# Gathers released in three batches a step instead of at eleven instructions, and a new order for the last steps of a graph attention kernel

## The chip, the cores and the metric

The kernel runs on one core of a Trainium2 chip. A core has five engines, each with an instruction queue of its own: TensorE (PE) for matrix products, VectorE (DVE) and ScalarE (ACT) for elementwise work, GpSimd (POOL), here used almost only to issue gathers, and SyncE (SP), which issues plain DMAs. They run side by side and meet at semaphores. The metric is device microseconds of one execution; lower is better.

## The reference

A graph attention layer over 3125 nodes of 128 features and 100000 edges sorted by destination; each edge has one of 5 relations, each relation its own weights for 8 heads of 16.

```python
for r in range(R):
    mask = edge_types == r
    q = jnp.einsum('eh,khd->ekd', x_dst, W_Q[r])
    k = jnp.einsum('eh,khd->ekd', x_src, W_K[r])
    v = jnp.einsum('eh,khd->ekd', x_src, W_V[r])
    logits = (q * k).sum(-1) / scale + attn_bias[r][None, :]
    ...
    exp_l = jnp.where(mask[:, None], jnp.exp(masked_logits - max_v[dst]), 0.0)
    sum_exp = jax.ops.segment_sum(exp_l, dst, num_segments=n)
    attn = exp_l / (sum_exp[dst] + 1e-12)
    out = out + jax.ops.segment_sum(attn[:, :, None] * v, dst, num_segments=n)
out = out.reshape(n, HIDDEN) @ out_proj_w.T + out_proj_b
h = out + node_embeddings
```

`h` is normalised over its features (with gamma and beta), the input is added, and the sum is normalised again.

## The kernel before

**Tiling.** Edges are cut into 782 tiles of 128 (`NTILE`), four tiles to a group, three groups to a step. There are 66 steps (`NST`); the first and the last have two groups. Before the loop, keys and values of all nodes and relations are computed and written to a table in HBM (`kv_d`). In the loop each tile needs the 128 rows of its edges' sources: one indirect DMA on the POOL queue, "a gather" (L836), which reads them into a ring of four steps (`kv_early` for three of them, `kv_late` for one). One tile in most steps needs no gather, since its rows are computed on PE (`early_*`, L1041 to L1067), so a step has 11 gathers; in all there are 719 at L836. Another 63 (L371) come before them.

**A step k of the loop** (L1375 on): `products` (L933) and `logits` (L991) on DVE use the gathered keys; `turn_logits` turns the scores on PE (L1023); `norm` (L1169 to L1173) and `relations` (L1209) finish step k-2; `spread_q` (L911) brings the queries of step k+1 to their edges; `weigh` (L1118) multiplies the gathered values of step k-1 with their weights; two scans (L1073, L1077) and `less_max` (L1087) take the maximum over each destination; `exps` (L1095) follows on ACT, `turn_exps` (L1102) on PE, and `weights` (L1112) on ACT ends the step. Between these stand three `places` on ACT (L1131, L1135: one-hot matrices of destinations) and three `sums` on PE (L1147, L1152: the sums over destinations of step k-1, one group each), taken by `place_next` and `sum_next`.

**The leaves.** The order of each engine's instructions is the order of the program, and a step writes it out by hand. POOL would run ahead as far as the ring lets it; what holds it is a leave. `gather(leave, n)` (L832) issues the next n gathers, and each of them waits for the instruction `leave`. `point(k, j, leave)` (L846) is called eleven times a step, j from 0 to 10, each time with an instruction that has just been written: j = 6 the products, 7 the copy `weights` of the step before (L1112), 8 the logits, 9 and 10 the first and last of `norm`, 0 the product of `weigh`, 1 the last matmul of `spread_q`, 2 and 3 the scans, 4 the DVE comparison of `spot`, 5 the last `places`. How many gathers are due is a formula:

```python
at = k + (j + 1) / POINTS
at += KV_LEAD - (KV_LEAD - KV_LOW) * min(max(at / (NST - 3), 0.0), 1.0)
```

All gathers of the steps up to `at` are issued, so the lead over the step that runs is 3 steps at the start and falls evenly to 2 at the end. (k, 6) to (k, 10) are called in the loop's iteration k+1, (k, 0) to (k, 5) in iteration k. In the text (k, j) is that point, and its gathers are its batch.

**The end.** After the loop the last step (`k = 65`, L1473 on) is written out: its products in two pieces (`piece`), `turn_logits`, `weigh` and `norm` of the steps before, the sums of steps 64 and 65 (`ahead_g`, `g`), and then the last three blocks of nodes (`rest`, 22 to 24): `project` (L1239), `residual` (L1266), `roots` (L1273, on ACT), `norms` (L1290 to L1318) and `store_z`.

Of the kernel before, what the change touches and what calls it, by code (L numbers as in the profile page):

```python
# [19 lines left out]
P = 128  # L20
# [126 lines left out]
def windowed_path(  # L147
# [177 lines left out]
    rsum = keep("rsum", [P, WN])  # L325
    lo = load.tile([1, NGR], F32, name="lo")
# [473 lines left out]
    qe = ps.tile([P, T * G3, H], F32, name="qe")  # L800
    fin = ps.tile([P, 4 * P], F32, name="fin")
# [30 lines left out]
    def gather(leave=None, n=1):  # L832
        for q in sum(tiles, [])[len(issued) :][: max(n, 0)]:
            ((kv, at, _),) = runs(q, q + 1)
            behind(
                nc.gpsimd.indirect_dma_start(  # L836
                    out=kv[:, at, :], out_offset=None, in_=kv_d[:, :],
                    in_offset=bass.IndirectOffsetOnAxis(
                        ap=idx[:, q % T, q // T : q // T + 1], axis=0
                    ),  # L840
                ),
                leave,
            )
            issued.append(q)

    def point(k, j, leave):  # L846
        at = k + (j + 1) / POINTS
        at += KV_LEAD - (KV_LEAD - KV_LOW) * min(max(at / (NST - 3), 0.0), 1.0)
        whole = min(int(at), NST)
        n = sum(len(t) for t in tiles[:whole])  # L850
        if whole < NST:
            n += int((at - whole) * len(tiles[whole]) + 1e-6)
        gather(leave, n - len(issued))
# [373 lines left out]
    def lifted(b):  # L1227
        n = min(P, N - b * P)
        nc.vector.tensor_tensor(
# [22 lines left out]
    def shifted(b):  # L1252
        n = min(P, N - b * P)
        if ("mv", b) not in live:
            live["mv", b] = pair()
            nc.vector.memset(live["mv", b], 0.0)
        xb = xn[:, b, :]
        nc.vector.tensor_tensor(xb[:n], xb[:n], beta_t[:n], op=ALU.add)

    def residual(b):  # L1260
# [4 lines left out]
        h = flow.tile([P, H], F32, name="h", bufs=1)  # L1265
# [4 lines left out]
    def roots(b, c0=0, c1=2, last=False):  # L1270
        sd = flow.tile([P, 2], F32, name="sd")
# [12 lines left out]
    def norms(b):  # L1284
# [30 lines left out]
        if b and c1 == 2:  # L1315
            n = min(P, N - (b - 1) * P)
            z = flow.tile([P, H], F32, name="z")
# [57 lines left out]
    for k in range(NST - 1):  # L1375
# [83 lines left out]
        sum_next()  # L1459
# [21 lines left out]
    live["lt", k] = lt = ps.tile([P, T * GE // 2], F32, name="lt")  # L1481
    for i in range(LASTG):
# [21 lines left out]
    weights(k)  # L1504
    sums(ahead_g[2])
    places(g[1])
    room = qe.rearrange("p n h -> p (n h)")
# [17 lines left out]
    f = starts(first, G0[k], G0[k + 1], ACTE)  # L1525
# [5 lines left out]
    sums(g[1])  # L1531
    last_norm(lt[:, None, :PW], lt[:WR, None, PW : PW + HEADS], n)
    project(rest[1])
# [521 lines left out]
```

## Time and profile before

| | us |
| --- | --- |
| median of 3 runs | 1020.38 |
| lowest and highest of them | 1020.12, 1023.06 |
| profiled execution, its own time | 1029.88 |
| span of the profiled execution | 1028.1 |

Times in the profile are counted from the first instruction of the profiled execution. PE is busy 92% of the span, DVE 87%, POOL 73%, ACT 69%. A row of the timeline gives start, duration, engine, line, operation, out<-in with shapes, how many instructions were merged (x), and in brackets the idle time of the engine before it and what ended that. "issue" means that nothing shown was waited for. In the groups of instructions the last columns are busy time, mean duration in ns, and idle time before with what ended most of it.

### The profile page before, as it was taken

The numbers are of one execution on the slowest core, as the hardware profiler recorded it, in microseconds if no ns is written. First come the engines' busy times: TensorE is split into PE (matmuls) and PEld (weight loads), VectorE is DVE, ScalarE is ACT, GpSimd is POOL, SyncE is SP. The second block draws the span as 40 slices with busy tenths as digits, with TensorE's granted clock in tenths as the row PEclk, the third lists the DMA queues.
The fourth block names the chain that finished last, engine by engine and source line by source line (L and its number), as shares of the span: only waits on it lengthen the run. The fifth ranks groups of instructions, "written<-read, shape, count | busy, mean of one in ns | idle before, by whom it ended". The sixth has DMA issues, their size and how long they took to land.

```text
span 1028.1 us, 21159 instructions
## 1 busy us (share of the span) xinstructions
PE 943.1 (92%) x6981; PEld 730.2 (71%) x6981; DVE 899.3 (87%) x1520; ACT 713.6 (69%) x1947; POOL 748.4 (73%) x793
## 2 busy tenths in 40 slices
PE   7995699999999999999999999999999999999896
PEld 3553578787777777777777777777777777777675
DVE  3665699899989998999999998999898999999895
ACT  2443368687777777777777777878777677877672
POOL 7777777777777777777777777777777777777730
PEclk9997599999999999999999999999999999999985
DMA  8997666666656666665666665666666566676620
GB/s 196 357 348 253 174 173 189 173 187 185 176 167 193 193 181 184 183 181 160 194 191 185 182 190 156 188 186 192 171 193 192 155 190 184 171 194 173 162 60 11
DMA packets 99077, 189.48 MB, mean 184 GB/s; under 512 B 19117, under 2 KB 59521, under 8 KB 98842
## 3 DMA queue, kind: packets, MB, share of 16 engines
q0 software_dynamic: 36528, 98.42, 37.8%
q1 hardware_dynamic: 61240, 88.74, 26.0%
q10 hardware_dynamic: 1194, 0.92, 0.4%
q8 instruction: 56, 0.92, 0.4%
q14 instruction: 59, 0.48, 0.2%
HBM read 157.61 MB, written 30.40 MB: 183 GB/s over the span
## 4 chain that ended last, share of the span: by engine, by line
DVE 35%; PE 26%; DMA 21%; issue 9%; ACT 4%; POOL 3%; DVEq 0%; ACTq 0%; SPq 0%; POOLq 0%
DMA kv_early<-kv_d,idx 14%; DVE qe L991 7%; PE both L1152 5%; DVE kv_early L933 5%; DMA kv_late<-kv_d,idx 5%; PE qe L911 4%; DVE wv L1118 4%; PE pr L508 3%; PE mid L1060 3%; POOL kv_early L836 3%; DVE run L1073 3%; DVE run L1077 3%; PE fin L1209 2%; DVE lx L966 2%; PE lt L1050 2%
## 5 line engine op out<-in xcount | busy, mean ns | idle before, releaser
L836 POOL DMA_INDIRECT kv_early<-kv_d,idx x543 | 515.9, 950 | 168.5 <-issue 85.9
L1152 PE MATMUL both<-wv,at 128*125 128x136 f32 x1552 | 269.4, 299 | 1.4 <-ACT at L1135 1.4
L1152 PEld LDWEIGHTS both<-wv,at 128*125 128x125 f32 x1552 | 207.9, 190 | 52.9 <-issue 46.0
L1131 ACT ACTIVATE at<-wide_at,nkey 128x125 f32<-128x125 f32 x776 | 245.0, 388 | 0.0
L836 POOL DMA_INDIRECT kv_late<-kv_d,idx x176 | 167.3, 950 | 53.6 <-issue 28.6
L1060 PE MATMUL mid<-wkv,xr 128*128 128x256 f32 x630 | 148.7, 383 | 1.6 <-ACT xr L1054 1.6
L911 PE MATMUL qe<-qw,hot 128*128 128x128 bf16 x2349 | 149.6, 225 | 0.0
L911 PEld LDWEIGHTS <-hot 128*128 128x128 bf16 x2352 | 145.4, 103 | 0.5 <-DVE vio L641 0.4
L1060 PEld LDWEIGHTS mid<-wkv,xr 128*128 128x128 f32 x630 | 116.4, 192 | 15.6 <-ACT xr L1054 2.0
L1135 ACT ACTIVATE at<-at 128x500 f32<-128x500 f32 x194 | 120.3, 620 | 6.1
L933 DVE TENSOR_TENSOR kv_early<-kv_early,qe 128x1536 f32<-128x1536 f32 (+3 forms) x70 | 89.2, 1275 | 25.9 <-DMA kv_early<-kv_d,idx 15.0
L1213 ACT COPY oT<-fin 128x25 f32 x194 | 35.1, 181 | 92.3 <-PE fin L1209 87.4
L1073 DVE TENSOR_TENSOR_SCAN run<-mk,lt 120x640 f32<-120x640 bf16 (+1 forms) x66 | 97.6, 1478 | 1.5 <-PE lt L1023 1.5
L1118 DVE TENSOR_TENSOR wv<-kv_early,mid 128x1536 f32<-128x1536 f32 (+2 forms) x51 | 86.2, 1692 | 12.4 <-PE mid L1060 9.3
L1077 DVE TENSOR_TENSOR_SCAN run<-lt,run 120x576 f32<-120x576 bf16 (+1 forms) x65 | 88.2, 1357 | 2.2
L991 DVE TENSOR_REDUCE qe<-kv_early 128x96 f32<-128x1536 f32 (+2 forms) x65 | 86.7, 1334 | 2.2
L1050 PE MATMUL lt<-diag,xg 128*128 128x512 f32 x252 | 84.1, 457 | 0.0
L1023 PE MATMUL lt<-ident,lx 128*120 128x128 f32 (+2 forms) x396 | 55.2, 277 | 26.8 <-DVE lx L966 10.7
L1023 PEld LDWEIGHTS lt<-ident,lx 128*120 128x120 f32 (+2 forms) x396 | 38.9, 137 | 55.7 <-ACT diag L1044 21.6
L1147 PE MATMUL both<-wv,over 128*5 128x136 f32 x386 | 77.3, 282 | 0.0
L1102 PEld LDWEIGHTS mid<-gather_heads,ls 120*128 120x128 f32 (+1 forms) x528 | 65.1, 194 | 15.0 <-ACT xTq L862 12.6
L1102 PE MATMUL mid<-gather_heads,ls 120*128 120x24 f32 (+1 forms) x528 | 67.4, 265 | 8.9 <-ACT xTq L862 7.5
(210 smaller groups left out, 1337.2 us busy)
## 6 DMA issues: line engine op xcount, KB each, us to landing
kt<-key_d SPq DMA_DIRECT2D x64, 384.0 KB
qw<-q_d SPq DMA_DIRECT2D x196, 96.0 KB
kv_d<-kvs SPq DMA_DIRECT2D x24, 640.0 KB
q_d<-q SPq DMA_DIRECT2D x25, 480.0 KB
mk<-msk_d SPq DMA_DIRECT2D x64, 150.5 KB
kv_early<-kv_d,idx POOLq DMA_INDIRECT x543
kv_late<-kv_d,idx POOLq DMA_INDIRECT x176
out<-z SPq DMA_DIRECT2D x24, 64.0 KB
```

Source lines behind the costliest of these rows:

```text
L836: nc.gpsimd.indirect_dma_start(out=kv[:, at, :], out_offset=None, in_=kv_d[:, :], in_offset=bass.IndirectOffsetOnAxis(ap=idx[:, q % T, q / ...
L911: spread = nc.tensor.matmul(dest[j], hot[:, j * P : (j + 1) * P], qw[:, c, :], start=(c == 0), stop=(c == 2),)
L933: made = nc.vector.tensor_tensor(kv[:, c0:c1, :H], kv[:, c0:c1, :H], qe[:, n:m], op=ALU.mult)
L991: made = nc.vector.tensor_reduce(lg[:, n : n + c1 - c0], heads(kv[:, c0:c1, :H]), AX.X, ALU.add)
L1060: nc.tensor.matmul(rows, xr[:, r * P : (r + 1) * P], wkv[:, r].rearrange("h s c -> h (s c)"), start=(r == 0), stop=(r == R - 1),)
L1073: there = nc.vector.tensor_tensor_scan(run[:n], mk[:n, 1 : WIDE + 1], lt, -BIG, op0=ALU.add, op1=ALU.max)
L1077: back = nc.vector.tensor_tensor_scan(run[:n, SEG:][:, ::-1], masks[:, SEG:][:, ::-1], run[:n, SEG:][:, ::-1], -BIG, op0=ALU.add, op1=ALU.max,
L1102: nc.tensor.matmul(ex.rearrange("p (i t) k -> p t i k", t=T)[:, t], ls[: n * LANES, t * P : (t + 1) * P], gather_heads[: n * LANES, :n], s ...
L1118: return nc.vector.tensor_tensor(heads(wv[:, a:b, :H]), heads(kv[:, at + a : at + b, H:]), ex[:, a:b, :, None].to_broadcast([P, b - a, HEA ...
L1131: nc.scalar.activation(at[:, t, :], row_at[:, :WR], AF.Abs, bias=nkey[:, t, g : g + 1], scale=1.0)
L1135: return nc.scalar.activation(at[:, :n], at[:, :n], AF.Relu, bias=1.0, scale=-1.0)
L1152: nc.tensor.matmul(pp[:WR], at[:, t, :], wv[:, T * i + t, :], start=(t == 0), stop=(t == end))
```

## The change

1. `point` returns at once unless j is 9, 1 or 7, and in `gather` only the first gather of a call gets the leave; the others follow it on POOL's queue. The formula for the number of gathers is as before.
2. In the last iteration of the loop (step 64) the third `sum_next` is left out, and two matmuls on a tile of zeros (`stir`) stand in its place. That group of sums comes after the loop, behind `turn_logits` and `weigh`.
3. After the loop the order is new: `norm`, `relations` and `by_node` of step 63 move behind the scans, the sums of step 64 come later, `places(g[1])` comes ahead of `weights`, `roots(begun)` behind the weighing.
4. The additions of `lifted`, and of `shifted` for the last three blocks, move from DVE to POOL and ahead of the pieces.
5. In the last blocks the second normalisation's roots are taken apart from the first's (`roots(b, 1, 2)` and `roots(b, 0, 1)`), both `residual`s come ahead of the `norms`, and some tiles get more buffers (`h` 2, `sd` 4, `z` 3).

```diff
+    still = keep("still", [P, 2 * P], BF16)
+    nc.vector.memset(still, 0.0)
...
                 leave,
             )
+            leave = None
             issued.append(q)
 
     def point(k, j, leave):
+        if j not in (9,1,7,):
+            return
...
+    def stir(n):
+        for _ in range(n):
+            nc.tensor.matmul(mid[:, P : 3 * P], still[:, :P], still, start=True, stop=True)
...
     def lifted(b):
         n = min(P, N - b * P)
-        nc.vector.tensor_tensor(
+        nc.gpsimd.tensor_tensor(
             ends[b - NT + len(ends)][:n], xn[:n, b, :], lift_t[:n], op=ALU.add
         )
...
     def shifted(b):
         n = min(P, N - b * P)
+        engine = nc.gpsimd if b >= begun else nc.vector
         if ("mv", b) not in live:
             live["mv", b] = pair()
-            nc.vector.memset(live["mv", b], 0.0)
+            engine.memset(live["mv", b], 0.0)
         xb = xn[:, b, :]
-        nc.vector.tensor_tensor(xb[:n], xb[:n], beta_t[:n], op=ALU.add)
+        engine.tensor_tensor(xb[:n], xb[:n], beta_t[:n], op=ALU.add)
...
         turn_exps(k)
         if soon:
             early_turn(k + 2, lt)
-        sum_next()
+        if k < NST - 2:
+            sum_next()
+        else:
+            stir(2)
...
+    shifted(begun)
+    for b in rest[1:]:
+        lifted(b)
+        shifted(b)
     for i in range(LASTG):
         piece(k, i)
     turn_logits(k)
     weigh(k - 1)
-    norm(k - 2)
-    relations(k - 2, fin[:, 3 * P :])
-    sums(ahead_g[0])
+    sum_next()
     places(ahead_g[1])
     places(ahead_g[2])
     places(g[0])
-    sums(ahead_g[1])
-    by_node(k - 2)
+    sums(ahead_g[0])
     scans(k)
     less_max(k)
+    sums(ahead_g[1])
     exps(k)
-    shifted(begun)
+    norm(k - 2)
     residual(begun)
-    for b in rest[1:]:
-        lifted(b)
-        shifted(b)
-    roots(begun, last=True)
     turn_exps(k)
+    relations(k - 2, fin[:, 3 * P :])
+    places(g[1])
     weights(k)
-    sums(ahead_g[2])
-    places(g[1])
...
     for i in range(LASTG):
         weigh(k, i, i + 1)
-    sums(g[0])
+    roots(begun, last=True)
+    by_node(k - 2)
+    sums(ahead_g[2])
     norm(k - 1)
-    relations(k - 1, fin[:, 3 * P :])
-    by_node(k - 1)
     norms(begun)
     store_z(begun - 1)
+    sums(g[0])
+    relations(k - 1, fin[:, 3 * P :])
+    f = starts(first, G0[k], G0[k + 1], ACTE)
+    by_node(k - 1)
+    roots(rest[1], 1, 2, last=True)
...
     sums(g[1])
+    project(rest[1])
     last_norm(lt[:, None, :PW], lt[:WR, None, PW : PW + HEADS], n)
-    project(rest[1])
+    norms(rest[1])
+    store_z(begun)
     last_nodes(mid[:, P:], 0, f[:n])
     last_nodes(lt[:, GE:], n, f[n:])
     residual(rest[1])
-    roots(rest[1], last=True)
+    roots(rest[1], 0, 1, last=True)
     project(rest[2])
+    residual(rest[2])
+    roots(rest[2], 0, 1, last=True)
     norms(rest[1])
-    store_z(begun)
-    residual(rest[2])
-    roots(rest[2], last=True)
+    norms(rest[2])
+    roots(rest[2], 1, 2, last=True)
+    roots(NT, 1, 2, last=True)
     norms(rest[2])
     store_z(rest[1])
-    roots(NT, 1, 2, last=True)
     norms(NT)
     store_z(rest[2])
```

More of the change, by code (lines that the diff above doesn't have):

```diff
@@ L800, in windowed_path @@
     qe = ps.tile([P, T * G3, H], F32, name="qe")
+    room = qe.rearrange("p n h -> p (n h)")
     fin = ps.tile([P, 4 * P], F32, name="fin")
@@ L1264, in residual @@
             xb = ends[b - NT + len(ends)]
-        h = flow.tile([P, H], F32, name="h", bufs=1)
+        h = flow.tile([P, H], F32, name="h")
         nc.vector.tensor_tensor(h[:n], live.pop(("pj", b))[:n], xb[:n], op=ALU.add)
@@ L1270, in roots @@
     def roots(b, c0=0, c1=2, last=False):
-        sd = flow.tile([P, 2], F32, name="sd")
+        sd = flow.tile([P, 2], F32, name="sd", bufs=4)
         if last:
@@ L1316, in norms @@
             n = min(P, N - (b - 1) * P)
-            z = flow.tile([P, H], F32, name="z")
+            z = flow.tile([P, H], F32, name="z", bufs=3)
             nc.vector.tensor_scalar(
@@ L1481, in windowed_path @@
     live["lt", k] = lt = ps.tile([P, T * GE // 2], F32, name="lt")
+    bank = 2 * P * T
+    live["both", k - 1] = room[:, bank : bank + G3 * (PW + HEADS)]
+    shifted(begun)
+    for b in rest[1:]:
+        lifted(b)
+        shifted(b)
     for i in range(LASTG):
@@ L1491, in windowed_path @@
     places(g[0])
-    sums(ahead_g[1])
-    by_node(k - 2)
+    sums(ahead_g[0])
     scans(k)
     less_max(k)
+    sums(ahead_g[1])
     exps(k)
-    shifted(begun)
+    norm(k - 2)
     residual(begun)
-    for b in rest[1:]:
-        lifted(b)
-        shifted(b)
-    roots(begun, last=True)
     turn_exps(k)
+    relations(k - 2, fin[:, 3 * P :])
+    places(g[1])
     weights(k)
-    sums(ahead_g[2])
-    places(g[1])
-    room = qe.rearrange("p n h -> p (n h)")
     live["both", k] = room[:, : G3 * (PW + HEADS + WN)]
@@ L1524, in windowed_path @@
     )
-    f = starts(first, G0[k], G0[k + 1], ACTE)
     n = LASTG - 1
```

## The prediction

> **What bounds the kernel now.** I read the page first: busy shares, slices, the two gather groups.
>
> ```profile
> span 1028.1 us, 21159 instructions
> PE 943.1 (92%) x6981; PEld 730.2 (71%) x6981; DVE 899.3 (87%) x1520; ACT 713.6 (69%) x1947; POOL 748.4 (73%) x793
> ...
> POOL 7777777777777777777777777777777777777730
> ...
> L836 POOL DMA_INDIRECT kv_early<-kv_d,idx x543 | 515.9, 950 | 168.5 <-issue 85.9
> ...
> L836 POOL DMA_INDIRECT kv_late<-kv_d,idx x176 | 167.3, 950 | 53.6 <-issue 28.6
> ```
>
> POOL looks 73% busy and free to spare. It is not: the share is the same in every slice, and the groups hold 719 gathers of 0.95 us with 222.1 us of idle time, 0.31 each. The question is whether that idle time is waiting. The timeline of POOL at the start, where the gathers of L371 have no leave at all, answers:
>
> ```profile
> 9.96 0.95 POOL L371 DMA_INDIRECT xg<-in_x,xi  x1 [0.30 <-issue]
> ```
>
> The same 0.30 us stands before a gather that waits for nothing. So 1.25 us is the pace of a gather, 11 gathers take 13.75 us, and POOL runs at that pace from 86 us (first L836) to 983 us, where the first longer gap comes. A step has 11 gathers; 719 of them at this pace are 899 us, the time from 86 to 985. **POOL is the bound; DVE waits for it in some of the steps**. In this one the last gather of the step starts at 953.28 and its products can start at 957.54, 4.3 us later:
>
> ```profile
> 953.28 0.95 POOL L836 DMA_INDIRECT kv_early<-kv_d,idx  x1 [0.30 <-DVE run L1077]
> ...
> 957.54 1.62 DVE L933 TENSOR_TENSOR kv_early<-kv_early,qe 128x1408 f32<-128x1408 f32 x1 [1.51 <-DMA kv_early<-kv_d,idx]
> ```
>
> A microsecond in which POOL stands still late in the loop is therefore a microsecond at the end.
>
> **The leaves.** What is removed costs nothing: the gap of 0.30 is there with and without a leave. What matters is whether the three leaves that stay come later than POOL does. By the formula of `point` the batch of j = 7 (about 6 gathers) now waits for the ACT copy L1112 that ends step k; its gathers had earlier leaves at points 2 to 7. The batch of j = 9 (2 gathers) waits for the first instruction of `norm`, that of j = 1 (3 gathers) for the last matmul of `spread_q`. I counted the gathers to find each batch's first one and compared its start with the end of its new leave. At the start, batch (1, 7) is the 45th gather (lines view up to it: 33 + 11):
>
> ```profile
> L836 POOL DMA_INDIRECT kv_early<-kv_d,idx x33 | 31.9, 968 | 10.1 <-issue 6.1 <-DMA kv_early<-kv_d,idx 1.2 <-DVE shut L589 0.6
> L836 POOL DMA_INDIRECT kv_late<-kv_d,idx x11 | 10.4, 947 | 3.4 <-issue 2.4 <-DVE wv L1118 0.3 <-DVE run L1073 0.3
> ...
> 134.55 0.24 ACT L1112 COPY wv<-mid 128x96 f32<-128x96 f32 x1 [1.16 <-PE mid L1102]
> ...
> 141.77 0.95 POOL L836 DMA_INDIRECT kv_early<-kv_d,idx  x1 [0.30 <-issue]
> ```
>
> The leave ends at 134.79, POOL arrives at 141.77: 7.0 us to spare, and the wait is free. But the lead falls from 3 steps to 2 over the loop, so the spare time shrinks. The same count at batch (50, 7), gather 576, and (62, 7), gather 706:
>
> ```profile
> L836 POOL DMA_INDIRECT kv_early<-kv_d,idx x432 | 410.7, 951 | 131.7 <-issue 65.8 <-DMA kv_early<-kv_d,idx 14.3 <-DVE both L1169 4.0
> L836 POOL DMA_INDIRECT kv_late<-kv_d,idx x143 | 136.0, 951 | 43.6 <-issue 21.3 <-DMA kv_late<-kv_d,idx 3.4 <-DVE qe L991 1.8
> ...
> 807.98 0.94 POOL L836 DMA_INDIRECT kv_early<-kv_d,idx  x1 [0.30 <-issue]
> 808.83 0.22 ACT L1112 COPY wv<-mid 128x96 f32<-128x96 f32 x1
> ...
> 915.66 0.95 POOL L836 DMA_INDIRECT kv_early<-kv_d,idx  x1 [0.30 <-issue]
> ...
> 918.18 0.24 ACT L1112 COPY wv<-mid 128x96 f32<-128x96 f32 x1 [0.90 <-PE mid L1102]
> ...
> 970.68 0.22 ACT L1112 COPY wv<-mid 128x96 f32<-128x96 f32 x1
> 970.79 0.94 POOL L836 DMA_INDIRECT kv_early<-kv_d,idx  x1 [0.30 <-DVE stats L1249]
> ```
>
> (50, 7): 809.05 against 807.98, POOL would be 1.1 us early. (62, 7): 0.1 early. Of these 13 batches 11 come out early, from 0.1 to 1.5 us, and (58, 7), the rows of 915.66 and 918.18, by 2.8. Behind a waiting gather stand all later ones, and DVE waits for those.
>
> **Sum of the loop.** If the leaves stayed where they are, POOL would be pushed back once, by the largest, 2.8 us. They don't stay: a pushed gather delays the products that wait for it, these delay the next ACT copy, and the next batch waits anew. I carried this through steps 50 to 63 with the trace's own times: a gather starts at the later of its predecessor plus 1.25 and its leave plus 0.15; products start at the later of the former step's DVE work and the landing of their last gather. Stalls of 1.2 (50), 0.3, 0.5, 0.1, 0.9 (55), 1.8 and 1.1 (58), 0.6 (59), 0.3 (61) add up to 6.7 us. Two of the late leaves, in 50 and 58, follow a stretch at half TensorE clock (windows view; columns: length, then busy PE, PEld, DVE, ACT, POOL, then granted clock, DMA share, GB/s):
>
> ```profile
> 800.20:803.60 3.40, 3.40 (x32) 3.40 (x30) 3.33 (x4) 2.38 (x8) 2.53 (x3) 0.50 0.47 100
> 909.40:912.80 3.40, 3.40 (x31) 3.40 (x31) 3.37 (x3) 2.38 (x9) 2.78 (x3) 0.50 0.69 218
> ```
>
> These need not recur; with the distance that other steps have from their products to L1112, the chain gives 4.4 to 5.6, by whether 0 or 0.3 us lie between a leave and its gather. Ends: 0, if later work takes up every stall, and 6.7. I take **+5.0**, since no POOL gap before 983 us is there to take up anything.
>
> The last gathers: before, the last ones are held back at no cost, since DVE is late.
>
> ```profile
> 987.56 0.95 POOL L836 DMA_INDIRECT kv_early<-kv_d,idx  x1 [3.01 <-DVE kv_early L933]
> ...
> 990.06 0.95 POOL L836 DMA_INDIRECT kv_early<-kv_d,idx  x1 [0.30 <-issue]
> 990.15 1.33 PE L911 MATMUL qe<-qw,hot 128*128 128x128 bf16 x21
> ...
> 996.24 0.54 DVE L933 TENSOR_TENSOR kv_early<-kv_early,qe 128x384 f32<-128x384 f32 x1
> ...
> 997.64 0.09 DVE L954 MEMSET lx<- 64x40 f32 x1
> ```
>
> The last one now waits for the matmuls that end at 991.48, starts near 991.6, and with the 4.3 us of the 953.28 row can be used at 995.9, before its use at 996.24: 0, at most 0.5.
>
> **The tail.** These rows carry it (timeline):
>
> ```profile
> 997.16 0.96 PE L1152 MATMUL both<-wv,at 128*125 128x136 f32 x6 [0.74 <-ACT at L1135]
> 999.17 1.32 PE L1023 MATMUL lt<-ident,lx 128*80 128x128 f32 x6
> 999.41 0.19 DVE L1169 TENSOR_SCALAR both<-both 125x24 f32<-125x24 f32 x1
> 1000.56 1.48 DVE L1073 TENSOR_TENSOR_SCAN run<-mk,lt 80x640 f32<-80x640 bf16 x1
> 1000.59 1.47 PE L1209 MATMUL fin<-rsum,o 125*128 125x25 f32 x6
> 1004.07 2.18 PE L1152 MATMUL both<-wv,at 128*125 128x136 f32 x8
> 1007.34 1.72 PE L1102 MATMUL mid<-gather_heads,ls 80*128 80x16 f32 x8
> 1009.34 1.28 DVE L1118 TENSOR_TENSOR wv<-kv_early,mid 128x512 f32<-128x512 f32 x2 [3.05 <-ACT wv L1112]
> 1017.36 0.63 PE L1239 MATMUL fin<-out_wT,oT 128*128 128x128 f32 x2
> ```
>
> PE works nearly without a pause from 997.16 to the projections at 1017.36; the exps turned at L1102 wait in its queue, not for DVE. The change takes a group of sums (997.16 to 999.0) out of the way of the scores and puts it behind them; the scores can start at 997.75 (end of L954) instead of 999.17, and with `norm` moved, the scans start up to 1.15 us earlier (999.41). But the exps still stand behind three groups of sums where two and L1209 stood: two of them took from 1002.06 to 1007.34, 2.65 us each, so 997.75 + 1.3 + 3 x 2.65 give 1007.0, about as before. L1209 (1.5 us) then comes behind them, ahead of the projections. At half clock that is about +1.4, and the new order of the last norms neither gains nor loses more than 0.3. At full clock PE has slack, the earlier scans count, and it is about -0.7. The additions moved to POOL ease a DVE that waits 3.05 us there: 0; POOL has been free since its last gather, 13 us earlier. The two matmuls of `stir` fill the pause of 0.74 ahead of the group that leaves: 0. The zero tile and the extra buffers cost at most a few tenths at the start. Tail: +1.4 to -0.7, I take **0**.
>
> Profiled execution: 1029.88 (span 1028.1 and 1.8 around it) + 5.0 + 0 = 1034.9. The median, 1020.38, is 9.5 lower; the same difference gives **1025.4 us**.
>
> **Rivals.** *The clock returns in the tail (the faster side).* The windows view:
>
> ```profile
> 977.70:981.10 3.40, 3.40 (x31) 3.40 (x31) 3.37 (x3) 2.25 (x9) 2.48 (x4) 0.50 0.32 98
> ...
> 994.70:998.10 3.40, 2.65 (x19) 2.06 (x18) 3.26 (x8) 3.37 (x11) 0.00 (x0) 1.00 0.00 0
> ...
> 1001.50:1005.00 3.50, 3.50 (x15) 2.79 (x16) 3.36 (x6) 2.43 (x8) 0.00 (x0) 0.50 0.03 7
> ```
>
> After a half-filled stretch the clock is 0.50 from 998.1 to the end, though PE is full; after the dense stretch at 977.7 it came back. Sums now run some 8 us on end instead of 5.5. If that lifts the clock near 1004, the PE work left up to 1018.0, 14 us, shrinks by 41% (0.27 us a pass in the 1004.07 row, 0.16 in the 997.16 row), 5.7, less some new waits: -5 against this profile. With +5 that is 1020.4; it decides for faster only if the loop loses under 2 us: 1015 to 1017. The Trainium skill, TensorE: Matmul & The Clock Gate, Part 1, says that the gate judges free-running windows of 3.4 us and opens after a busy one; by that, 8 us always hold a whole window, 5.5 us only by luck. The trace agrees with the length (the half-clock stretches above last 3.4) but shows that a full PE alone isn't enough. For it: the median is 9.5 below this profile, so other executions may already have the clock; then it isn't a gain.
>
> *The leaves don't bind* (the change does nothing in the loop): only the tail, 1019.7 to 1021.8. For: POOL is late up to step 49. Against: 11 of 13 batches after it.
>
> *The stalls grow:* every step from 50 pays 0.7 us or more and the last batch is late: +9, 1029.5.
>
> **Chances.** Forecast 0.57 (own range 1022.5 to 1028), clock 0.20, no binding 0.14, growth 0.09. About 0.3% (3.1 us) is what a measurement can tell from no change: slower needs over 1023.4, nearly all of forecast and growth: 0.62; faster, below 1017.3, is half of the clock case: 0.10; the same 0.28. Range: 1017.5 to 1029.5, with 0.05 left out below and 0.1 above.
>
> **What would show it.** In the changed profile POOL's gaps before L836 stay at 0.30 up to about 800 us and then show some nine of 0.5 to 2 us, released by ACT L1112 and PE L911, in sum 5 (without the last five gathers); the scans of the last step start about 1.1 us earlier after its products; L1102 doesn't, unless the clock is 1.0 there. Wrong it is if POOL never waits, or waits and DVE's gaps before L933 swallow it.

## The result and the profile after

| | before | after |
| --- | --- | --- |
| time, median of 5 runs (us) | 1020.74 (1020.12 to 1023.96) | 1033.68 (1028.04 to 1034.55) |
| ratio, 95% interval | | 1.0104 [1.0081, 1.0128] |
| profiled execution (us) | 1029.88 | 1028.04 |

The change costs 13 us by the medians, where 5 were forecast. The profiled execution of after is the shortest of its five; the other four took 1032.93 to 1034.55 at mean granted clocks of 0.964 to 0.960, the profiled one had 0.969. The profiled execution of before is none of its five, and 9.1 us longer than their median. So the two profiles differ by -1.8 us and the medians by +12.9, and both have to be explained. The chips of all runs behind this section take about 1300 us for the kernel before, not 1020, so what they show is compared only within them.

**The loop after.** The timeline of GpSimd, the rows on which the forecast rests (start, duration, and in brackets the idle time before it and what ended it):

```profile
725.36 0.94 POOL L839 DMA_INDIRECT kv_early<-kv_d,idx  x1 [0.83 <-ACT wv L1118]
...
807.36 0.95 POOL L839 DMA_INDIRECT kv_early<-kv_d,idx  x1 [0.30 <-issue]
...
912.96 0.94 POOL L839 DMA_INDIRECT kv_late<-kv_d,idx  x1 [0.78 <-PE qe L917]
...
917.93 0.94 POOL L839 DMA_INDIRECT kv_early<-kv_d,idx  x1 [1.53 <-ACT wv L1118]
...
942.51 0.94 POOL L839 DMA_INDIRECT kv_early<-kv_d,idx  x1 [1.16 <-PE qe L917]
...
974.08 0.95 POOL L839 DMA_INDIRECT kv_early<-kv_d,idx  x1 [0.30 <-issue]
```

GpSimd now waits for the copy (L1112 before, L1118 now) and for the last matmul of `spread_q` (L911, now L917). Gather 576 starts at 807.36 (807.98 before), gather 706 at 974.08 (970.79 before): 0.6 us ahead has become 3.3 us behind. Counted over the whole loop, without the last five gathers, nine gaps are longer than 0.45 us, from 0.48 to 1.53, and they hold 5.1 us beyond the usual 0.30. The first of them stands before gather 511. Up to there the changed execution had been ahead, as one product and gather 510 show (before, then after; the product at 960.29 is the one that stands at 957.54 in the profile of before):

```profile
682.72 1.62 DVE L933 TENSOR_TENSOR kv_early<-kv_early,qe 128x1408 f32<-128x1408 f32 x1 [0.36 <-DMA kv_late<-kv_d,idx]
...
725.32 0.95 POOL L836 DMA_INDIRECT kv_early<-kv_d,idx  x1 [0.30 <-issue]
```

```profile
680.83 1.62 DVE L939 TENSOR_TENSOR kv_early<-kv_early,qe 128x1408 f32<-128x1408 f32 x1
...
723.59 0.95 POOL L839 DMA_INDIRECT kv_early<-kv_d,idx  x1 [0.30 <-issue]
...
960.29 1.62 DVE L939 TENSOR_TENSOR kv_early<-kv_early,qe 128x1408 f32<-128x1408 f32 x1 [1.52 <-DMA kv_early<-kv_d,idx]
```

GpSimd goes from 1.7 us ahead at gather 510 to 3.3 behind at gather 706: 5.0 us, the sum of the gaps. The eight large products from 627 to 723 us start 0.7 to 2.2 us earlier than before, all of those from 943 us on start 2.5 to 2.8 us later.

**The tail after.** The timeline again, then two stretches of it (length, busy time of PE, PEld, DVE, ACT, POOL, granted clock, DMA share, GB/s):

```profile
998.82 0.54 DVE L939 TENSOR_TENSOR kv_early<-kv_early,qe 128x384 f32<-128x384 f32 x1
...
1001.87 1.47 DVE L1079 TENSOR_TENSOR_SCAN run<-mk,lt 80x640 f32<-80x640 bf16 x1
...
1006.89 1.04 PE L1108 MATMUL mid<-gather_heads,ls 80*128 80x16 f32 x8 [1.31 <-ACT kv_early L1137]
...
1015.52 0.63 PE L1249 MATMUL fin<-out_wT,oT 128*128 128x128 f32 x2
```

```profile
993.00:996.40 3.40, 3.40 (x27) 3.15 (x24) 3.37 (x3) 2.41 (x9) 1.18 (x2) 0.50 0.13 39
...
1000.00:1003.40 3.40, 3.06 (x22) 2.31 (x23) 3.37 (x5) 3.34 (x10) 0.00 (x0) 1.00 0.00 0
```

The last products end 2.6 us later than before (999.36 against 996.78). Since DVE too had been ahead, by 1.6 us in the mean of those eight products, some 4.2 of the 5.1 us lost on GpSimd reached it, and 2.6 are left against before. Why this execution was ahead until then is not shown; 0.3 us of it stand already at the first gather of the loop (85.68 against 86.00). From there to the end it is 26.9 us instead of 31.3. The scans follow the products' start by 3.05 us instead of 4.32, and the clock is 1.0 from 996.4 to 1013.5, where the profile of before has 0.5 from 998.1 to the end. It came back at 996.4, before the last products had ended and so before TensorE came to any of the new order (`stir`, at 999.26). Both executions have full clock for 17.1 us ahead of the last drop (981.1 to 998.1 before); in after this stretch lies later. How much of the 4.4 us is the new order's own is not shown. 2.6 - 4.4 = -1.8: that is the difference of the two profiles.

### The profile page after: what moved, and what is told of

Its sections match the earlier page's. It is cut to its first block, busy times and chain, and to the rows that moved or that the text cites. A ratio compares the mean times of both kernels' runs of the same rounds, so it can differ in the third digit from the quotient of the medians.

```text
span 1026.3 us, 20719 instructions
## 1 busy us (share of the span) xinstructions
PE 936.8 (91%) x6983; PEld 724.8 (71%) x6983; DVE 900.1 (88%) x1516; ACT 714.0 (70%) x1949; POOL 748.8 (73%) x800
## 4 chain that ended last, share of the span: by engine, by line
DVE 29%; PE 28%; DMA 17%; POOL 12%; issue 10%; ACT 3%; DVEq 0%; ACTq 0%; POOLq 0%
DMA kv_early<-kv_d,idx 13%; POOL kv_early L839 10%; DVE qe L997 6%; PE both L1158 6%; PE qe L917 5%; PE pr L510 5%; DVE kv_early L939 5%; DVE wv L1124 3%; DMA kv_late<-kv_d,idx 3%; DVE run L1079 2%; PE fin L1219 2%; DVE run L1083 2%; PE mid L1066 2%; DVE lx L972 2%; PE lt L1056 2%
## 5 line engine op out<-in xcount | busy, mean ns | idle before, releaser
L1158 PE MATMUL both<-wv,at 128*125 128x136 f32 x1528 | 262.5, 297 | 0.3 <-ACT at L1141 0.3
L1158 PEld LDWEIGHTS both<-wv,at 128*125 128x125 f32 x1528 | 202.7, 188 | 50.1 <-issue 44.4
L917 PE MATMUL qe<-qw,hot 128*128 128x128 bf16 x2349 | 150.3, 226 | 0.0
L917 PEld LDWEIGHTS <-hot 128*128 128x128 bf16 x2352 | 145.6, 104 | 0.6 <-DVE vio L643 0.4
```

Of the source, the lines that this page charges most:

```text
L917: spread = nc.tensor.matmul(dest[j], hot[:, j * P : (j + 1) * P], qw[:, c, :], start=(c == 0), stop=(c == 2),)
L1158: nc.tensor.matmul(pp[:WR], at[:, t, :], wv[:, T * i + t, :], start=(t == 0), stop=(t == end))
```

## The experiments

On the chips of these 18 runs the kernel before has medians of 1301.6 to 1333.6 us, with the same program and, on DVE and ACT, the same duration of single instructions. Each ratio is against runs of the kernel before on the same chip. Why these chips take longer was not known when the first runs were planned; it is told where it came out.

### Which part of the change costs

The leaves alone (`e1_points`: the early return of `point` and the one leave of a batch, old tail), the tail alone (`e2_tail`), and both kernels again. The leaves are this:

```diff
+            leave = None
             issued.append(q)
     def point(k, j, leave):
+        if j not in (9,1,7,):
+            return
```

> The kernel before with the change of point and gather alone (leaves at j = 9, 1, 7, only the first gather of a call gets one); the end as before. Theory A (the loop loses all of it: the stalls of POOL are longer in undisturbed executions than the 7 us that the profile of the changed kernel shows): +12 to +13 us, ratio 1.012. Theory B (the loop loses about 5 us as forecast, the rest is lost in the tail): +5 us, ratio 1.005; POOL's gaps over 0.45 us before the last five gathers add up to 4 to 7 us and none is earlier than 700 us.

> The kernel before with all of the change but the leaves: eleven points, each gather with its leave, the new order at the end, stir, additions on POOL. Theory A: within 1 us of before. Theory B: +7 to +8 us, ratio 1.007, and the profile shows where: either PE at half clock from the last step to the end (then the span after the last gather is 36 us or more), or, at full clock, a wait in the chain of the last blocks.

> The kernel before again, for the granted clock of its executions. If theory B is right by way of the clock, executions of about 1020 us show a mean clock above the 0.961 of the profile shown before (1029.9 us), by 0.008 or more; if the clock has no part, they show 0.961 too.

> The changed kernel again, for a second profile and clocks. Theory B by way of the clock: executions of 1033 us have a mean clock about 0.008 below that of the 1028 us profile, and a profile of one shows half clock through the tail; the sum of POOL's extra gaps before the last five gathers stays at 5 to 8 us. Theory A: the extra gaps grow to 12 us in a slow execution.

| kernel | time (us) | ratio, 95% interval |
| --- | --- | --- |
| e1_points | 1412.65 | 1.0632 [1.0578, 1.0687] |
| e2_tail | 1334.36 | 0.9986 [0.9943, 1.0028] |
| e0_before | 1333.44 | 1.0036 [0.9995, 1.0077] |
| e0_after | 1412.43 | 1.0643 [1.0563, 1.0722] |

The leaves carry the loss. The new tail shows no difference, within an interval of -8 to +4 us. What the expectations of e0_before and e0_after say of executions of 1020 to 1033 us can't be judged, as none came. The tail alone was run once more:

> All of the change but the leaves. Theory T (in the first measurement the loop lost about 5 us and the tail the rest, because the TensorE clock stays at half in the tail of the changed kernel in most executions, while the kernel before usually gets it back): on a chip on which before takes about 1020 us this runs at 1026 to 1030, with L1105-like turned exps and projections at half clock to the end. Rival L (the tail is free, the whole 13 us comes from the three late leaves): 1018 to 1022. On a chip on which before takes about 1330 us both give a ratio of 0.995 to 1.005, as the run e2_tail did, and this run settles nothing between them.

1302.15 us, 1.0037 [0.9995, 1.0079]: again none that is clear of noise (-1 to +10 us). As its expectation says, on such a chip it can't decide between its theories.

### Is it the shrinking lead?

The forecast says that the leaves come too late because the lead falls from 3 steps to 2. So it was kept at 3, for the leaves alone and for the whole change, and in another run the copy (j = 7) was exchanged for j = 4, the first DVE instruction of `spot`:

```diff
-KV_LOW = 2.0
+KV_LOW = 3.0
```

```diff
-        if j not in (9,1,7,):
+        if j not in (9,1,4,):
```

> The leaves alone again (j = 9, 1, 7, one leave a call), to see them beside the next three kernels on one chip. Theory P (POOL stands still before leaves that come too late, above all the copy L1112): if before runs near 1020 us, +5 to +13 us and POOL gaps released by ACT L1112 or PE L911; if before runs near 1333 us as in the last call, +6% as there. Theory Q (batches cost by themselves: gathers in a burst land later): the same times, but DMA landings later and no gaps of POOL released by the leaves.

> The leaves alone, and the lead kept at 3 steps to the end (KV_LOW = 3.0): batches as before, but each gather's leave comes up to a step earlier. Theory P: the loss goes, within 0.3% of before or faster, POOL's gaps released by leaves under a fifth of those of e1b. Theory Q: the loss stays as in e1b.

> The whole change with the lead kept at 3 steps. Theory P: as e3, and the tail adds between -3 and +1 us, so no slower than before by more than 0.3%. Theory Q: as slow as the changed kernel.

> As e1b, with j = 4 in place of j = 7 (leave of that batch: the DVE comparison of spot, some 3 us before L1112; a batch of 3 gathers at j = 4 and 5 at j = 9). Theory P: most of the loss goes, under a third of e1b's. Theory Q: the loss stays above two thirds, since the batches are as large.

| kernel | time (us) | ratio, 95% interval |
| --- | --- | --- |
| e1b_points | 1409.43 | 1.0640 [1.0620, 1.0659] |
| e3_lead3 | 1417.88 | 1.0704 [1.0679, 1.0729] |
| e5_after_lead3 | 1417.97 | 1.0711 [1.0690, 1.0733] |
| e4_941 | 1300.97 | 0.9820 [0.9772, 0.9869] |

More lead does not help, it even costs 0.6%. Three other leaves, also in three batches, are faster than the eleven. So on these chips the lead is not the cause, and neither is the number of batches.

### Why these chips take longer

The page of the kernel before on these chips (e0_before), its busy times and its most idle TensorE group, and two rows of its timeline:

```profile
span 1331.4 us, 21159 instructions
...
PE 1053.4 (79%) x6981; PEld 802.1 (60%) x6981; DVE 911.5 (68%) x1520; ACT 714.3 (54%) x1947; POOL 744.3 (56%) x793
...
L1060 PE MATMUL mid<-wkv,xr 128*128 128x256 f32 x630 | 220.1, 516 | 144.9 <-ACT xr L1054 131.1
L1152 PE MATMUL both<-wv,at 128*125 128x136 f32 x1552 | 282.7, 309 | 5.7 <-issue 2.9
```

```profile
500.80 0.97 PE L1102 MATMUL mid<-gather_heads,ls 120*128 120x24 f32 x8
...
507.23 0.24 ACT L1112 COPY wv<-mid 128x96 f32<-128x96 f32 x1 [4.97 <-remote]
```

DVE and ACT work about as long as in the first measurement (911 and 714 us against 899 and 714), but no engine is the bound: GpSimd is busy 56%. The copy L1112 needs the matmuls of L1102, which end at 501.77; it starts at 507.23, and nothing in the page releases it ("remote"). In the trace's records of semaphores TensorE's next update after 499.5 stands at 507.21, with the two after it at 507.27 and 507.38, though their matmuls ended at 502.93 and 504.39. The updates come late and in a bunch. I counted them two ways: *late* is the time from the end of a matmul that updates the semaphore to the next recorded update, where that is over 1.2 us; *still* is the sum of stretches over 2 us in which TensorE, DVE and ACT together record no update (from 150 us on). The first measurement has one of each in before (2 and 3 us); e0_before has 94 late ones, 310 us in sum, and 96 still stretches, 328 us.

Span 1331 against 1028 is a difference of 303 us, but neither sum is the time lost. Records are missing on these chips: for the 929 matmuls that update TensorE's semaphore, e0_before has 776 updates on record, before 923, and a matmul whose own update has no record counts as late. Counted from the last matmul ahead of each recorded update, which leaves most such cases out, e0_before has 44 late updates, 93 us in sum, and before none. And TensorE, DVE and ACT are all idle at once for only 52 us (0 in before), from 150 us to 35 us before the end. TensorE alone is busy 110 us longer than the 943.1 us of the first measurement, with the same matmuls, at a mean clock of 0.875 against 0.961. So the sums show that updates hang; what the 303 us are made of they don't tell.

### Set of leaves against number of batches

> Four leaves of a step instead of three: those of j = 9, 1, 4 and 7, with the old order of the last steps. Theory S (on a chip on which before takes about 1330 us the loss of 6% comes from the leave of j = 7, the ACT copy that waits for a late TensorE semaphore once a step; any set with it in loses): ratio 1.03 to 1.07. Rival R (it is the number and size of the batches; 9, 4, 1 gained because its batches are more even): ratio 0.97 to 0.99. On a chip on which before takes 1020 us, the theory of the shrinking lead gives +3 to +4 us against before, as the batch of j = 7 is then only three gathers.

> The changed kernel with the leave of j = 7 replaced by that of j = 4 (the first DVE instruction of spread of step k + 2). If leaves and tail add up, on a chip on which before takes about 1330 us: ratio 0.975 to 0.99, as e4_941 alone gave 0.982 and the tail 0.999. Theory R2 (what e4_941 gained was a chance of one placement and shifts with any other edit): ratio 0.99 to 1.03. On a chip on which before takes 1020 us the leave of j = 9 then comes too late for its five gathers and the loop loses 13 us, ratio about 1.013 to 1.02.

Four leaves, j = 9, 1, 4 and 7: 1341.69 us, 1.0349 [1.0260, 1.0438]. The changed kernel with 9, 4, 1: 1268.48 us, 0.9788 [0.9721, 0.9856]. The gain of e4_941 keeps with another tail, so R2 falls, and this version is faster than the kernel before, and so than the changed one, which loses 6% on these chips. The set with the copy in it loses, as theory S says; but the same numbers could come from something simpler, the lengths of the runs in which GpSimd issues gathers with no pause (gap over 0.45 us). In e4_941 they are of 5 and 6 gathers, in the set of four often 9 (29 times), and in e1_points 8 and 3, as its timeline shows:

```profile
709.72 0.95 POOL L836 DMA_INDIRECT kv_late<-kv_d,idx  x1 [2.35 <-PE qe L914]
710.97 0.95 POOL L836 DMA_INDIRECT kv_late<-kv_d,idx  x1 [0.30 <-issue]
712.23 0.95 POOL L836 DMA_INDIRECT kv_late<-kv_d,idx  x1 [0.30 <-issue]
719.60 0.95 POOL L836 DMA_INDIRECT kv_late<-kv_d,idx  x1 [6.42 <-ACT wv L1115]
```

The batch of j = 9 finds its leave long past and runs on behind that of j = 7: six and two gathers make one run of eight (719.60 to 729.3), then come the three of j = 1.

### Do the gathers hold up the semaphores?

Four versions of the kernel before: pauses of GpSimd after every third gather (fills of an idle tile of 128x512); half the bytes of each gather; a second buffer for the keys, so that SyncE loads them earlier; no leaves. The second leaves the values half of each tile at zero, and the old row numbers point at half rows, so only its time counts.

```diff
             issued.append(q)
+            if len(issued) % 3 == 0:
+                for _ in range(3):
+                    nc.gpsimd.memset(idle, 0.0)
```

```diff
-                    out=kv[:, at, :], out_offset=None, in_=kv_d[:, :],
+                    out=kv[:, at, :H], out_offset=None, in_=kv_d.rearrange("n (c h) -> (n c) h", h=H),
```

```diff
-        live["kt", k] = kt = ahead.tile([P, TB * P], BF16, name="kt", bufs=1)
+        live["kt", k] = kt = ahead.tile([P, TB * P], BF16, name="kt", bufs=2)
```

```diff
-                leave,
+                None,
             )
             issued.append(q)
```

> The kernel before, with three GpSimd fills of 128x512 (an idle tile) after every third gather, some 1.5 to 2 us in which no gather is issued. On these chips TensorE's semaphores arrive 1.2 to 7 us after the matmul that sends them, about 100 times in a run (310 us in sum in e0_before, once in the first measurement), and most of them 1.0 to 1.6 us after the end of a gather. Theory G (gathers issued back to back hold these semaphores up; a set of leaves is good or bad by where it puts the pauses of GpSimd): the sum of the late semaphores falls below 200 us, and the time falls too, ratio 0.90 to 0.98. Rival Q (the load of keys and query rows by SyncE holds them up) and rival N (neither; it is a state of the chip): the sum stays at 280 to 340 us, ratio 1.00 to 1.04, since the gathers now need 18 us of a step.

> The kernel before, with gathers that bring 128 instead of 256 numbers a row, so that the values half of each tile stays zero and half of the gathered bytes are left out; as many gathers are issued at the same places. If the bytes in flight hold up the semaphores (theory G by traffic): sum of the late ones below 200 us, ratio 0.88 to 0.96. If it is the issuing of gathers (theory G by issue), or rivals Q and N: sum 280 to 340 us, ratio 0.99 to 1.01.

> The kernel before, with two buffers for the keys, so that their load of 384 KB starts a step's part earlier and no longer together with the query rows. Rival Q (in the kernel before the late semaphores lie 1 to 5 us behind the issue of the key load, while it and the query rows are in flight): the sum falls below 200 us, ratio 0.90 to 0.97. Theories G and N: 280 to 340 us, ratio 0.98 to 1.02.

> The kernel before, with no leave at all: gathers in the same order, held only by the reuse of their tiles. Theory G by issue: GpSimd runs in longer bursts, sum of late semaphores above 340 us, ratio 1.03 to 1.08. Rival Q and N: ratio 0.99 to 1.01. Theory S (the leave of the ACT copy, j = 7, carries the loss through the chain copy, gathers, products): without it and the others ratio 0.97 to 1.00.

| kernel | time (us) | ratio, 95% interval | late (us) | still (us) |
| --- | --- | --- | --- | --- |
| p1_pause3 | 1415.77 | 1.0876 [1.0819, 1.0934] | 220 | 83 |
| p2_half | 1316.50 | 1.0144 [1.0075, 1.0213] | 317 | 278 |
| p3_kt2 | 1297.75 | 0.9962 [0.9901, 1.0023] | 319 | 278 |
| p4_noleave | 1766.89 | 1.3540 [1.3442, 1.3637] | 469 | 678 |

Neither fewer bytes nor another time for SyncE's load changes the late updates: traffic by bytes and rival Q fall. That half the bytes take 1.4% longer, where at most 1% was expected, stayed unexplained. With no leaves the kernel loses 35%, far more than any theory said. Its timeline shows one step (gathers, one matmul, and the ACT cast that needs it), and the windows view the stretches of it:

```profile
910.29 0.94 POOL L836 DMA_INDIRECT kv_early<-kv_d,idx  x1 [11.41 <-DVE wv L1118]
...
912.99 0.59 PE L868 MATMUL fin<-wq,xTq 128*128 128x256 f32 x2
...
919.73 0.37 ACT L873 CAST q<-fin 128x256 bf16<-128x256 f32 x1 [7.21 <-remote]
...
922.80 0.95 POOL L836 DMA_INDIRECT kv_early<-kv_d,idx  x1 [0.30 <-issue]
...
937.04 0.94 POOL L836 DMA_INDIRECT kv_early<-kv_d,idx  x1 [13.29 <-DVE wv L1118]
```

```profile
910.20:913.70 3.50, 3.50 (x42) 3.08 (x39) 3.43 (x4) 2.29 (x8) 2.80 (x3) 1.00 0.32 70
913.70:923.80 10.10, 1.45 (x11) 0.83 (x9) 4.18 (x14) 0.90 (x2) 7.61 (x9) 0.73 0.68 191
926.20:937.00 10.80, 10.50 (x58) 8.43 (x59) 4.13 (x8) 7.44 (x21) 0.00 (x0) 0.73 0.11 46
```

Eleven gathers run without a pause from 910.3 to 923.8. For 3.5 us the others work on; then TensorE is busy 1.45 of 10.1 us and ACT 0.90. When GpSimd is silent, TensorE is busy 10.50 of 10.80. This step is 26.8 us long (910.29 to 937.04): the work of the others and the run of gathers hardly overlap.

The pauses of p1 remove three quarters of the stillness (328 to 83 us), as theory G has it, and a third of the late updates (310 to 220; expected was below 200). Counted from the last matmul ahead of each update, nearly all late ones go: 5 us in sum instead of 93, where p2_half and p3_kt2 keep 88 and 84 and p4_noleave has 390. TensorE, DVE and ACT are all idle at once for 10 us instead of 52, in p4_noleave for 371. The time rises all the same, against the expectation of theory G, because the pauses were too long: the page shows GpSimd as the bound.

```profile
L848 POOL MEMSET idle<- 128x512 f32 x717 | 381.4, 532 | 27.7
...
702.38 0.95 POOL L837 DMA_INDIRECT kv_early<-kv_d,idx  x1 [0.18 <-PE qe L915]
...
707.72 0.95 POOL L837 DMA_INDIRECT kv_early<-kv_d,idx  x1 [0.18 <-issue]
```

Three gathers now take 5.34 us, eleven 19.6, and a step takes 19.6 in the mean.

### Pauses instead of leaves, and shorter pauses

No leaves but the pauses of p1; one fill instead of three in the kernel before; the same in the changed kernel with leaves 9, 4, 1.

> No leave at all, but three fills of GpSimd (1.9 us with the gap behind them) after every third gather, as in p1_pause3. Theory G by issue (what leaves do on these chips is to break up runs of gathers, and any pause does it): the loss of p4_noleave (1767 us) goes, and the time is GpSimd's own pace as in p1_pause3, 3 x 1.25 + 1.6 = 5.3 us for three gathers, 19.6 us a step: ratio 1.07 to 1.12; late or missing stretches of semaphores as few as there. Rival (the order that leaves impose on gathers and the other engines is what counts, p4 lost 35% for want of it): ratio 1.20 to 1.38.

> The kernel before with one fill of GpSimd (0.53 us, then 0.18 us of gap) after every third gather, so that 11 gathers need about 15.7 us, less than the step of 17.8 us. Theory G, if pauses of 0.7 us are long enough: ratio 0.93 to 0.98. Theory G with pauses that have to last longer (semaphores came 1.0 to 1.6 us after the end of a gather): 0.99 to 1.02. Rival (a busier GpSimd only costs): 1.02 to 1.09.

> The changed kernel with leaves 9, 4 and 1 (ratio 0.979 in f3_after_941) and the one fill after every third gather. If short pauses help: ratio 0.92 to 0.97; if they don't, 0.98 to 1.01; if they only cost GpSimd time, above 1.01.

| kernel | time (us) | ratio, 95% interval | late (us) | still (us) |
| --- | --- | --- | --- | --- |
| r1_noleave_pause3 | 1411.73 | 1.0884 [1.0791, 1.0978] | 221 | 68 |
| r2_pause1 | 1268.93 | 0.9795 [0.9712, 0.9878] | 341 | 181 |
| r3_after_941_pause1 | 1274.67 | 0.9858 [0.9755, 0.9962] | 348 | 169 |

r1 decides between theory G and the order of the gathers. Without one leave, the pauses alone bring 1767 us back to 1412, the time that p1 has with all its leaves; the late updates counted from the last matmul go from 390 us to 4. What holds the kernel without leaves up is its unbroken runs of gathers, and a pause does for it what leaves do. One fill is enough to beat the kernel before by 2%; on top of the leaves 9, 4, 1 it adds nothing. By the longest runs that occur often the ratios are: 11 gathers 1.354, 9 among shorter ones (f2) 1.035, 8 (e1_points) 1.063, 5 and 6 (e4_941) 0.982, at most 3 with short pauses (r2) 0.980. That is no strict order: f2 and e1_points stand the wrong way round, and the kernel before, with runs of mostly 1 to 6 and a few longer, is slower than e4_941. Nor do the late updates rank them: r2 has more (341 us) than e0_before and is faster, and counted from the last matmul f3_after_941 has as much (96 us against 93) and is faster too. Run length explains the large loss of p4; for the differences of 2% it is a guess.

### Where the 6% of the leaves sit

Longer runs don't by themselves make e1_points stand still longer: its still stretches sum to 218 us, less than the 328 of e0_before, and its late updates to 307 (135 counted from the last matmul, against 93). What grows is TensorE's work. The page of e1_points:

```profile
span 1409.6 us, 20701 instructions
...
PE 1122.7 (80%) x6981; PEld 838.7 (60%) x6981; DVE 907.5 (64%) x1520; ACT 713.2 (51%) x1947; POOL 745.5 (53%) x793
...
L1155 PE MATMUL both<-wv,at 128*125 128x136 f32 x1552 | 351.8, 365 | 8.7 <-issue 6.0
L914 PE MATMUL qe<-qw,hot 128*128 128x128 bf16 x2349 | 192.7, 225 | 192.5 <-issue 180.1
...
L1063 PE MATMUL mid<-wkv,xr 128*128 128x256 f32 x630 | 149.2, 384 | 2.4 <-issue 2.4
```

The span is 78 us longer than that of e0_before, and TensorE is busy 69 us longer with the same matmuls. Its pause, once a step, has moved: 145 us of idle time ahead of L1060 (now L1063) are down to 2, and 193 stand ahead of L914. With it the half clock moved: the matmuls of L1060 are shorter by 71 us in sum, the sums (L1152, now L1155) longer by 69, and the rest, L914 and what follows it, longer by 71. The clock's stretches at half number about the same from 160 us on (56 and 54), but 37 of the 56 last one stretch of 3.41 us in e0_before, and 35 of the 54 last two to five in e1_points; in sum 273 and 386 us, which is worth up to 57 of the 69 us (an estimate: half of the difference, if TensorE is busy all the time). Four neighbouring windows of one such stretch, in e1_points:

```profile
708.30:711.72 3.42, 2.61 (x11) 1.99 (x12) 1.08 (x4) 0.00 (x0) 1.70 (x2) 0.50 0.52 79
711.72:715.13 3.41, 3.41 (x11) 2.34 (x11) 0.43 (x2) 1.67 (x5) 1.15 (x2) 0.50 0.82 262
715.13:718.54 3.41, 3.41 (x16) 2.70 (x15) 3.34 (x6) 1.60 (x5) 0.00 (x0) 0.50 0.11 39
718.54:721.95 3.41, 3.41 (x11) 2.38 (x11) 2.21 (x4) 1.18 (x3) 1.90 (x2) 0.50 0.14 38
```

In the second and third row TensorE is busy from end to end, and the clock stays at 0.50. The fourth, 2.5 us of it matmuls of 512 columns (L1053), ends the stretch at 721.95. Behind the pause of e0_before come the long matmuls of L1060 (256 columns to a weight load), and there one full window brings the clock back (rows of the windows view):

```profile
510.45:513.86 3.41, 3.41 (x13) 2.42 (x11) 0.79 (x1) 1.66 (x3) 1.68 (x2) 0.50 0.51 166
513.86:517.20 3.34, 3.34 (x49) 3.27 (x49) 3.31 (x3) 2.20 (x9) 0.99 (x2) 1.00 0.13 34
```

That the half clock makes the 69 us is read from these rows; no run held the clock and moved the pause alone.

## Why the prediction was wrong

**The bound, right.** In the first measurement GpSimd issues the gathers of the loop at 1.25 us in both kernels, and DVE waits for it.

**The leaves, right, in mechanism and size.** Nine gaps of up to 1.5 us, nearly all released by the ACT copy and by `spread_q`, 5.1 us in sum; the forecast was some nine and 5. Three of them stand already at 725 to 766 us, before step 50. Between such a leave and its gather lie 0.27 us as a rule, where the forecast took 0.15 and allowed up to 0.3. Two of the last five gathers wait, 3.25 and 2.22 us, and that costs nothing, as expected: the products at 998.82 start without a gap. "No POOL gap before 983 us is there to take up anything" held as well, since some 4.2 of the 5.1 us reached DVE. That only 2.6 are left at the end comes from the lead of 1.7 us that this execution had before the first stall, which the sum could not know.

**The tail.** The scans come 1.3 us earlier after the products (forecast 1.1). The tail was put at 0 and is 4.4 us shorter in that profile. It looks like the rival "the clock returns in the tail", but its mechanism isn't there: the clock came back at 996.4, ahead of the new order, and not near 1004 by a longer run of sums. That was luck of this execution. On the chips of the experiments the tail alone made no difference that could be seen, 0.9986 and 1.0037.

**The step that failed: "the same difference gives 1025.4".** For an execution like the profiled one the forecast was 1034.9, and four of the five executions took 1032.93 to 1034.55. That these lie near it is no proof of the sum, as none of them was seen in a profile. From this 9.5 us were taken off, because before's median lies that much below its profile, as if after's executions would have the same luck. They don't: 9.5 us down were forecast, and after's median lies 5.6 us above its own profile. 12.9 = -1.8 between the profiles + 9.1 from before's profile down to its median + 5.6 from after's profile up to its median. The prediction named the reason in passing ("other executions may already have the clock; then it isn't a gain") and did not draw the conclusion: then the median of before may be free of a penalty that the changed kernel can run into.

How large such a penalty can be is shown by the tails of the experiments, from the end of the last products to the end, with one and the same code (windows view, one row for each kernel: p1_pause3, then e0_before, then p3_kt2):

```profile
1388.20:1419.40 31.20, 22.25 (x90) 16.91 (x90) 18.74 (x58) 11.13 (x35) 0.00 (x0) 0.52 0.03 10
```

```profile
1301.20:1331.40 30.20, 20.45 (x90) 15.51 (x90) 18.91 (x58) 11.52 (x35) 0.00 (x0) 0.58 0.03 10
```

```profile
1271.45:1296.05 24.60, 13.60 (x90) 10.06 (x90) 18.55 (x58) 11.41 (x35) 0.00 (x0) 0.86 0.04 12
```

The same 90 matmuls need 22.25 us at a mean clock of 0.52 and 13.60 at 0.86, and the tail 31.2 or 24.6 us. Over all profiles the old tail has two forms, 24.6 to 25.7 us in eight and 30.2 to 31.4 in five, the profile of before among these with 31.3. The new tail takes 25.5 to 28.9 in seven, so it saves up to 5.9 us against the long form and costs 0.9 to 4.2 against the short one.

That before's five timed executions had the short form, and four of after's five a long new tail, would go the way of the two offsets, but it does not cover them: 31.3 - 24.6 is 6.7 of the 9.1 us, and 28.9 - 26.9 is 2.0 of the 5.6. after's clocks say the same. At a span of 1031 us each 0.005 less is 10 us more at half clock, so 0.964 to 0.960 against 0.969 means 10 to 19 us more, and the longest new tail (f1_tail, 28.9 us at 0.68) has only 6 us more of half clock than that of after (26.9 at 0.76). The rest must lie ahead of the tail. No execution of before at 1020 us and none of after at 1033 was seen in a profile, and no chip of the experiments took 1020 us. So the step that failed is known, the clock of the tail is a likely part of it by argument, and the cause of some 8 us (12.9 less the 4 to 5 of the leaves) stays open.

**The rivals.** "Leaves don't bind" fell in both places. "Stalls grow" (+9, 1029.5) is nearest in time and wrong in mechanism: the stalls did not grow. What no rival had is a chip on which the leaves matter for another reason, 6% instead of 0.5.

## What to carry to other kernels

A profile belongs to one execution: where it lies 9 us from the median, find out what the median does not have before carrying a difference over, since a change can keep or lose that as well. Where a queue of gathers is the bound, thinning its leaves costs what each leave is late; where it isn't, the same leaves set the lengths of its runs, and these can cost more than the waits. Leaves 9, 4, 1 or a short pause gain 2% on the chips of the experiments, but a pause of 0.42 us more for three gathers (3.75 to 4.17 us in r2_pause1) would cost some 100 us where GpSimd sets the pace, an estimate from 240 such groups that no run here tried.

## What the runs showed of the hardware

On the chips of the experiments a long run of gathers issued back to back lets TensorE's semaphore updates through late and in bunches, 5.4 us late in the rows of e0_before; in the step shown of p4_noleave TensorE and ACT all but stop 3.5 us after the run began (busy 1.45 and 0.90 of 10.1 us). Counted from the last matmul ahead of each update, the late ones sum to 390 us in p4_noleave, and to 4 in r1_noleave_pause3, where pauses of 1.9 us follow every three gathers. Pauses of 0.7 us after three gathers (r2_pause1) lower the stillness from 328 to 181 us, 1.9 us to 68 to 83 (r1_noleave_pause3, p1_pause3). Halving the bytes doesn't lower the late updates. In the first measurement 719 gathers run almost without a pause, and one update is late. What makes the chips differ, and by what path gathers hold up an update, stayed open.

The granted clock does not follow TensorE's busy share. In the tail of before four windows of 3.41 us, busy from end to end and mostly with sums, kept 0.50 (1001.5 to 1015.2; two of them below), while in e0_before a window busy for 2.90 us of it ended the half clock (last row; 1.0 from 278.3 on):

```profile
1004.93:1008.34 3.41, 3.41 (x16) 2.70 (x15) 1.28 (x8) 1.53 (x2) 0.00 (x0) 0.50 0.00 0
1008.34:1011.75 3.41, 3.41 (x15) 2.70 (x15) 1.28 (x2) 1.21 (x4) 0.00 (x0) 0.50 0.00 0
```

```profile
274.90:278.31 3.41, 2.90 (x7) 2.37 (x8) 1.34 (x5) 3.35 (x8) 1.34 (x3) 0.50 0.67 225
```

The Trainium skill, TensorE: Matmul & The Clock Gate, Part 1, has the clock return after one busy window of about 3.4 us. The length agrees with the stretches here; that any busy window suffices does not, and the measurement decides.
